# Weight codes of a decoder layer turned into weights on GpSimd instead of ScalarE

## The chip, the cores and the metric

One core of a Trainium2 chip runs the whole layer as one program. The metric is the device time of one execution in microseconds (us). TensorE (PE in the profile, PEld for its weight loads) multiplies, VectorE (DVE), ScalarE (ACT) and GpSimd (POOL) do the element-wise work, and SyncE (SP) issues DMAs. Each engine works off its own queue in order; an instruction waits for semaphores of others.

## The reference

A decoder layer on `x` of 2 x 512 x 1024 floats, in three parts, each with a residual:

```python
x = x + attn(layernorm(x))           # q, k, v, o weights from 4-bit codes
x = x + fq(layernorm(x)) @ fq(ctx)   # both sides rounded to 8-bit steps
x = x + layernorm(x) @ binarized(weight).T

# in attn: codes are int32 from 0 to 15, one scale per 128 rows and column
w = (codes.astype(float32) - 8.0) * repeat(scales, 128, axis=0)
q, k, v = x @ wq, x @ wk, x @ wv     # 32 query heads, 8 key/value heads of 128
# rotary embedding on even and odd elements of q and k, causal softmax, then
out = heads @ wo                     # 4096 x 1024 codes
```

## The kernel before

**Tiles.** The 1024 tokens lie along the free side, 512 for each batch. A column tile is one head's 128 columns of the query, key or value codes: 8 groups of 128 rows, brought as int32 by one DMA (`fetch_w`, L283, tile `st`) and turned into float32r weights `w` by subtracting 8 on ScalarE. There are 32 query, 8 key and 8 value tiles. Query and key tiles are turned in two halves (L294), the even and the odd columns, which puts the pairs of the rotary embedding in separate halves; a value tile takes one instruction (L291). A head's 128 rows of the output projection (`load_wo`, L304, tiles `sto` and `wo`) take one instruction too (L309).

**Scales.** They are not multiplied into the weights. A projection's sum `z` in PSUM is rescaled between two groups by the ratio of their scales (L368, on ScalarE, in place), and the last scale enters when the sum is read. So TensorE's group g+1 waits for ScalarE's L368 after group g. Each product is made of two passes, with the high and the low part of the input (`yH`, `yL`, L316).

**Around it.** Query and key sums are rotated by VectorE (L333 to L337). Attention of a head and batch: scores (L451), masked minimum on VectorE (L461), exponential on ScalarE (L466), division on VectorE (L470, L471), transposes (L493) copied by ScalarE (L498), values (L509), split into a high and a low part (L517, L519). The output projection (L316, `zo`, one PSUM buffer) is added into `accT` by VectorE (L432). Beside this the context is quantized and the last part's weight binarized on VectorE (L550 to L552, L579 to L587); their DMAs are issued by GpSimd (L564, L568, L577, L596) and wait for VectorE or ScalarE there. The later parts (from about 1000 us) read them back.

**Buffers and order.** `st` has 2 buffers, shared by column and output codes; `w` has 3, `wo` 2. The order of the steps is a written time line: `put(start, length, thunks)` places them at fractions of a unit (one head and batch), and a load stands LEAD = 0.7 units before its projection. From the sorted line a scheduler makes each engine's queue. The first three column tiles (`FIRST`: key 0, value 0, query 0) are loaded by hand at the start:

```python
sts = [fetch_w(*kc) for kc in FIRST[:2]]
...
ws[FIRST[0]] = load_w(*FIRST[0], sts[0])
...
ws[FIRST[1]] = load_w(*FIRST[1], sts[1])
projection(*FIRST[2])[0]()
```

Of the kernel before, what the change touches and what calls it, by code (L numbers as in the profile page):

```python
# [14 lines left out]
AF = mybir.ActivationFunctionType  # L15
ALU = mybir.AluOpType
# [7 lines left out]
HH = HD // 2  # L24
# [17 lines left out]
def decoder_layer(  # L42
# [20 lines left out]
    nc = tc.nc  # L63
# [217 lines left out]
    def fetch_w(kind, c):  # L281
        st = stp.tile([P, NK, HD], I32, tag="st", name="st")
        nc.sync.dma_start(st, codes[kind][:, :, c * HD : (c + 1) * HD])  # L283
        return st

    def load_w(kind, c, st=None):

        st = fetch_w(kind, c) if st is None else st
        w = wp.tile([P, NK, HD], F32R, tag="w", name="w")
        if kind == 2:  # L290
            nc.scalar.activation(w, st, AF.Copy, bias=-8.0)  # L291
        else:
            for e in range(2):
                nc.scalar.activation(  # L294
                    w[:, :, e * HH : (e + 1) * HH],
                    st.rearrange("p g (e two) -> p g two e", two=2)[:, :, e],
                    AF.Copy,
                    bias=-8.0,
                )
        return w  # L300

    def load_wo(h):
        st = stp.tile([P, D], I32, tag="st", name="sto")
        nc.sync.dma_start(st, o_codes[h * HD : (h + 1) * HD, :])  # L304
        if h == NH - 1:
            w = kvp.tile([P, D], F32R, tag="kT", name="wo")
        else:
            w = wop.tile([P, D], F32R, tag="wo", name="wo")
        nc.scalar.activation(w, st, AF.Copy, bias=-8.0)  # L309
        return w  # L310

    def product(z, lhsT, high, low, first=True, last=True):
# [30 lines left out]
    def projection(kind, c, bs=tuple(range(B))):  # L343
# [54 lines left out]
        def load():  # L398
            ws[kind, c] = load_w(kind, c)
# [20 lines left out]
    def out_projection(h):  # L420


        def tile_of(o):
            def run():
                hl = [[oHL[h, b][i] for b in range(B)] for i in range(2)]
                z = ps_z.tile([P, T], F32, tag="zo", name="zo", bufs=1)
                product(z, wo[h][:, o * P : (o + 1) * P], hl[0], hl[1])
                s = so[:, o, h : h + 1]
                if h == 0:
                    nc.scalar.activation(accT[o], z, AF.Copy, scale=s)  # L430
                else:
                    nc.vector.scalar_tensor_tensor(  # L432
                        accT[o], z, s, accT[o], ALU.mult, ALU.add
                    )

            return run

        def load():
            wo[h] = load_wo(h)

        return load, [tile_of(o) for o in range(NO)]
# [200 lines left out]
    ratios(sc1, ratio1, last1)  # L642
    turned[2][0]()
    ws[FIRST[0]] = load_w(*FIRST[0], sts[0])
    turned[2][1]()
    turned[3][0]()
    turned[3][1]()
    ws[FIRST[1]] = load_w(*FIRST[1], sts[1])
    projection(*FIRST[2])[0]()
    load_input(6)  # L650
# [305 lines left out]
```

## Time and profile before

| | before |
|---|---|
| median of three runs | 1229.86 us (1229.81 to 1230.28) |
| profiled execution, its span | 1229.79 us, 1228.0 us |
| granted TensorE clock | 0.994 |
| PE, DVE, ACT, POOL busy | 1189.5, 988.6, 856.5, 36.9 us |
| conversions of codes, on ACT | 88 of column tiles (60.2 us), 32 of the output projection (33.8 us) |

A row of the groups reads: line, engine, operation, what it writes and reads, shape and count, then busy time, mean duration of one in ns, the engine's idle time before it, and what ended that. TensorE's busy time is modelled and overlaps itself, so 97% does not mean that it never waits. A line of the waits reads: who waited for whom, microseconds in total, times, longest.

### The profile page before, as it was taken

Reading aid. Unit: us, or ns where it says so; the run is one execution under the profiler, and the core shown is the slowest. Engines: PE = TensorE matmul, PEld = TensorE weight load, DVE = VectorE, ACT = ScalarE, POOL = GpSimd, SP = SyncE. Lnnn points to the kernel's source line nnn. Section 1 sums busy time; section 2 is a strip of 40 time slices with the busy share of each in tenths; the row PEclk is TensorE's granted clock in tenths of the full one; section 3 lists DMA queues with packets and bytes.
Section 4 is the critical chain, followed back from the end, with each engine's and each line's share of the span. In section 5 each row is a group of like instructions: output and inputs, shape, how many; then the busy total and the mean of one; then the engine's idle time right before and its main releaser. Section 6 shows DMA issues by size and latency. Waiting matters only on the chain.

```text
span 1228.0 us, 14707 instructions
## 1 busy us (share of the span) xinstructions
PE 1189.5 (97%) x5022; PEld 801.2 (65%) x5030; DVE 988.6 (81%) x2035; ACT 856.5 (70%) x1767; POOL 36.9 (3%) x79
## 2 busy tenths in 40 slices
PE   5899999999999999999999999999999989899998
PEld 3557676667676777777767776777777666555443
DVE  6767889999999798979897889798979898955620
ACT  6899987877878777787778777877787744512310
POOL 1000000000000000000000000000000000000000
PEclk9999999999999999999999999999999989999999
DMA  7022222222122121212121212121212073110001
GB/s 246 1 92 85 69 69 86 69 69 65 56 71 85 61 78 44 69 61 77 61 77 44 69 61 78 61 76 45 69 61 73 25 239 102 42 36 35 18 24 45
DMA packets 75500, 85.69 MB, mean 70 GB/s; under 512 B 3073, under 2 KB 60801, under 8 KB 75425
## 3 DMA queue, kind: packets, MB, share of 16 engines
q1 hardware_dynamic: 69344, 63.64, 16.5%
q0 software_dynamic: 6080, 21.11, 4.7%
q8 instruction: 39, 0.64, 0.2%
q14 instruction: 37, 0.30, 0.1%
HBM read 72.16 MB, written 12.58 MB: 69 GB/s over the span
## 4 chain that ended last, share of the span: by engine, by line
PE 84%; DVE 8%; ACT 6%; issue 1%; DMA 1%; SPq 0%; POOL 0%; ACTq 0%
PE z L316 26%; PE zo L316 17%; PE o L509 11%; PE s L451 10%; PE m L875 9%; PE t L493 6%; ACT z L368 3%; PE m L843 2%; DVE accT L432 2%; DVE rot L333 1%; PE zb L316 1%; DVE accT L412 1%; DMA accT<-in_x 1%; PE vps L393 1%; DVE p L471 1%
## 5 line engine op out<-in xcount | busy, mean ns | idle before, releaser
L368 ACT ACTIVATE z<-z,ratio 128x512 f32<-128x512 f32 x672 | 423.7, 675 | 75.2 <-PE z L316 74.0
L316 PE MATMUL z<-yH,w 128*128 128x512 f32 x768 | 348.9, 460 | 7.8 <-ACT z L368 5.1
L432 DVE SCALAR_TENSOR_TENSOR accT<-zo,so,accT 128x1024 f32<-128x1024 f32 x224 | 286.5, 1279 | 55.7 <-PE zo L316 54.0
L316 PE MATMUL z<-yL,w 128*128 128x512 f32 x768 | 313.5, 416 | 0.0
L316 PEld LDWEIGHTS z<-yH,w 128*128 128x128 f32 x768 | 144.5, 189 | 92.0 <-ACT z L368 60.1
L316 PE MATMUL zo<-oH,wo 128*128 128x512 f32 x464 | 200.5, 432 | 1.4 <-DVE accT L432 0.8
L316 PE MATMUL zo<-oL,wo 128*128 128x512 f32 x464 | 184.7, 398 | 0.0
L466 ACT ACTIVATE p<-p,low 128x128 f32<-128x128 f32 (+3 forms) x256 | 143.9, 565 | 54.7 <-DVE low L461 51.8
L451 PE MATMUL s<-kT,q 128*128 128x128 f32 (+3 forms) x512 | 173.6, 439 | 0.0
L316 PEld LDWEIGHTS z<-yL,w 128*128 128x128 f32 x768 | 145.3, 189 | 25.7 <-issue 7.2
L509 PE MATMUL o<-pt,v 128*128 128x512 f32 (+3 forms) x512 | 149.9, 434 | 0.1
L333 DVE SCALAR_TENSOR_TENSOR rot<-z,last,sin 64x512 f32<-64x512 f32 x160 | 120.0, 750 | 23.3 <-PE z L316 19.8
L509 PEld LDWEIGHTS o<-pt,v 128*128 128x128 f32 x512 | 96.3, 189 | 60.3 <-issue 30.7
L461 DVE CUSTOM_DVE_ANT_0 p<-s,mask 128x128 f32<-128x128 f32 (+3 forms) x256 | 121.2, 482 | 14.8 <-PE s L451 13.4
L498 ACT COPY pt<-t 128x512 f32<-128x512 f32 (+3 forms) x256 | 105.4, 442 | 21.6 <-PE t L493 20.5
L493 PE MATMUL t<-ident,p 128*128 128x128 f32 x640 | 117.3, 278 | 2.7 <-DVE oL L519 2.0
L316 PEld LDWEIGHTS zo<-oH,wo 128*128 128x128 f32 x464 | 87.3, 188 | 42.9 <-DVE accT L432 22.7
L875 PE MATMUL m<-bwT,y2T 128*128 128x512 f32 x256 | 111.3, 592 | 0.0
L451 PEld LDWEIGHTS s<-kT,q 128*128 128x128 f32 x512 | 89.5, 190 | 28.7 <-ACT pt L498 2.3
L493 PEld LDWEIGHTS t<-ident,p 128*128 128x128 f32 x640 | 79.3, 141 | 36.4 <-ACT pt L498 8.1
L316 PEld LDWEIGHTS zo<-oL,wo 128*128 128x128 f32 x464 | 87.6, 189 | 17.1 <-issue 2.6
L471 DVE TENSOR_SCALAR p<-p,inv 128x128 f32<-128x128 f32 (+3 forms) x256 | 95.3, 382 | 2.3
(129 smaller groups left out, 1050.8 us busy)
## 6 DMA issues: line engine op xcount, KB each, us to landing
st<-in_L_attn_q_codes SPq DMA_DIRECT2D x32, 512.0 KB, 4.0
sto<-in_L_attn_o_codes SPq DMA_DIRECT2D x32, 512.0 KB, 3.3
ctx<-in_ctx POOLq DMA_DIRECT2D x16, 512.0 KB, 3.6
accT<-in_x SPq DMA_DIRECT2D x8, 512.0 KB, 6.3
st<-in_L_attn_k_codes SPq DMA_DIRECT2D x8, 512.0 KB, 3.7
st<-in_L_attn_v_codes SPq DMA_DIRECT2D x8, 512.0 KB, 3.8
wt<-in_L_ffn_weight POOLq DMA_DIRECT2D x8, 512.0 KB, 3.8
bwd<-wT POOLq DMA_DIRECT2D x8, 512.0 KB, 2.9
```

Of the source, the lines that this page charges most:

```text
L316: nc.tensor.matmul(z[:, b * S : (b + 1) * S], lhsT, rhs[b], start=first and part == 0, stop=last and part == 1, skip_group_check=True,)
L333: nc.vector.scalar_tensor_tensor(t[to], z[of_], s[of_], sin[of_], ALU.mult, ALU.mult)
L368: nc.scalar.activation(z, z, AF.Copy, scale=ratio_[:, g + 1 : g + 2])
L432: nc.vector.scalar_tensor_tensor(accT[o], z, s, accT[o], ALU.mult, ALU.add)
L451: nc.tensor.matmul(ps[:, :n], q[:, b * S + i * P : b * S + n], k[:, b * S : b * S + n], start=True, stop=True,)
L461: nc.vector.tensor_tensor_reduce(p[:, :n], ps[:, :n], mask[:, S - n :], -1.0, -MASKED, ALU.add, ALU.min, accum_out=low,)
L466: nc.scalar.activation(p[:, :n], p[:, :n], AF.Exp, bias=low, scale=-1.0, accum_out=total)
L471: nc.vector.tensor_scalar(p[:, :n], p[:, :n], inv, None, ALU.mult)
L493: nc.tensor.transpose(ps[:, (i - j) * P : (i - j + 1) * P], probs[h, b][i][:, j * P : (j + 1) * P], ident,)
L498: nc.scalar.copy(ptq[h, b][j], ps[:, :n])
L509: nc.tensor.matmul(ps[:, j * P :], v[:, b * TB + j, :], pt[j], start=(j == 0), stop=(j == TB - 1),)
L875: nc.tensor.matmul(ps, yTs[m][:, k, :], late["bwT"][:, k, c], start=(k == 0), stop=(k == NK - 1))
```

## The change

The conversions are issued to GpSimd, as an addition of -8 and a multiplication by 1, where the tile was not fetched beforehand; all of the output projection's are. The split in halves stays. Behind `load_w` every line stands one lower in the changed kernel (L316 is L317 there, L368 is L369); the conversions are its L298, L300 and L310.

```diff
     def load_w(kind, c, st=None):
 
+        early = st is not None
         st = fetch_w(kind, c) if st is None else st
         w = wp.tile([P, NK, HD], F32R, tag="w", name="w")
         if kind == 2:
-            nc.scalar.activation(w, st, AF.Copy, bias=-8.0)
+            parts = [(w, st)]
         else:
-            for e in range(2):
-                nc.scalar.activation(
-                    w[:, :, e * HH : (e + 1) * HH],
-                    st.rearrange("p g (e two) -> p g two e", two=2)[:, :, e],
-                    AF.Copy,
-                    bias=-8.0,
-                )
+            both = st.rearrange("p g (e two) -> p g two e", two=2)
+            parts = [(w[:, :, e * HH : (e + 1) * HH], both[:, :, e]) for e in range(2)]
+        for to, codes_ in parts:
+            if early:
+                nc.scalar.activation(to, codes_, AF.Copy, bias=-8.0)
+            else:
+                nc.gpsimd.tensor_scalar(to, codes_, -8.0, 1.0, ALU.add, ALU.mult)
         return w
 
     def load_wo(h):
...
-        nc.scalar.activation(w, st, AF.Copy, bias=-8.0)
+        nc.gpsimd.tensor_scalar(w, st, -8.0, 1.0, ALU.add, ALU.mult)
         return w
```

## The prediction

> **What bounds the kernel now.** I read the page first: busy time and the chain that ended last.
>
> ```profile
> PE 1189.5 (97%) x5022; PEld 801.2 (65%) x5030; DVE 988.6 (81%) x2035; ACT 856.5 (70%) x1767; POOL 36.9 (3%) x79
> PE 84%; DVE 8%; ACT 6%; issue 1%; DMA 1%; SPq 0%; POOL 0%; ACTq 0%
> ```
>
> TensorE (PE) carries 84% of the path, and no edit here touches it. What an engine swap can win or lose lies in the 6% on ScalarE (ACT, 74 us) and the 8% on VectorE (DVE, 98 us). Then the busy time by stretch (columns: PE, PEld, DVE, ACT, POOL, each with its count, then clock and DMA):
>
> ```profile
> 60.00:100.00 40.00, 37.84 (x153) 23.79 (x152) 29.89 (x75) 39.72 (x83) 1.60 (x3) 1.00 0.28 85
> 100.00:140.00 40.00, 39.97 (x184) 28.75 (x182) 29.71 (x64) 39.45 (x77) 1.08 (x2) 1.00 0.24 78
> 400.00:700.00 300.00, 299.38 (x1307) 214.73 (x1305) 258.04 (x532) 236.76 (x504) 8.62 (x16) 1.00 0.20 64
> ```
>
> ScalarE is full from 60 to 140 us (79.2 of 80). In the long middle it is 79% busy (237 of 300), VectorE 86%, and GpSimd (POOL) idle. Next the groups by shape: what moves, the rows nearest to its new price, and VectorE's largest group that works from SBUF to SBUF.
>
> ```profile
> L294 ACT ACTIVATE w<-st 128x512 fp32r<-128x512 int32 x80 | 51.6, 678 | 7.4 <-PE z L316 5.7 <-DMA st<-in_L_attn_k_codes 1.3
> L309 ACT ACTIVATE wo<-sto 128x1024 fp32r<-128x1024 int32 x32 | 33.8, 1056 | 4.0 <-PE zo L316 4.0
> L291 ACT ACTIVATE w<-st 128x1024 fp32r<-128x1024 int32 x8 | 8.6, 1069 | 2.3 <-PE z L316 2.3
> L805 POOL TENSOR_SCALAR v<-mv 128x1 f32<-128x1 f32 x8 | 1.8, 221 | 196.0 <-DVE mv L92 196.0
> L77 POOL MEMSET mask<- 128x384 f32 x1 | 0.4, 422 | 0.0
> masks.py:30 POOL TENSOR_SCALAR_AFFINE_SELECT mask<-mask 128x128 f32<-128x128 f32 x1 | 0.3, 312 | 0.0
> L471 DVE TENSOR_SCALAR p<-p,inv 128x512 f32<-128x512 f32 x64 | 30.9, 482 | 1.0
> ```
>
> Last, who waits: TensorE's weight loader for ScalarE's rescaling in 60 to 140 us, the same in 140 to 990 us (total, times, longest), and then all that TensorE waited for the paired conversions of L294 in the whole run.
>
> ```profile
> PEld z L316 <- ACT z L368: 6.8, 20, 0.9
> ...
> PEld z L316 <- ACT z L368: 40.2, 138, 0.7
> ...
>   PEld z L316: 1.9, 3
>   PE z L316: 0.6, 1
> ```
>
> The weights themselves are hardly ever late. What is late is the rescaling L368, which shares ScalarE with the conversions.
>
> **What moves.** Only tiles handed in with their codes stay on ScalarE. That is two tiles, the first key and value tile: the third of FIRST is loaded by its projection without codes, so it goes to GpSimd although the change is said to spare three. Moved are 32 query and 7 key tiles in two halves each (78 instructions), 7 value tiles and 32 output tiles (39 of 128x1024). ScalarE loses 78 x 0.678 + 7 x 1.069 + 32 x 1.056 = 94 us by the mean durations.
>
> **What ScalarE's relief is worth.** On the chain, window by window, the moved conversions make eleven pieces, 8.1 us in all (59.28, 80.74, 191.9, 242.26, 340.35, 378.7 and 979.1 us among their starts). By stage:
> - 20 to 60 us: the third tile's conversion ends on ScalarE at 24.52 and TensorE uses it at 24.57. Its codes are requested at 16.60 and such a transfer takes 4.0 us, so GpSimd can finish near 22.5. Behind it ScalarE's rescalings are next late: 0.5 us won, at most 1.1.
> - 60 to 140 us: 10.35 us of conversions leave a full ScalarE (5.92 + 3.30 + 1.13). TensorE's waits on ScalarE there come to about 11 us, but it is itself close to full after 100 us. I take half, 5 us; bounds 0 and 10. Here weights have little lead (the tile at 80.62 is used at 81.91), so a slower conversion shows: 1 us back.
> - 140 to 990 us: 78.2 us leave (42.41 + 29.44 + 6.36), 12% of ScalarE's work. TensorE waits for ScalarE here for some 55 us (40.2 for L368, the rest for copies). In proportion 12% of it, 6.5 us, is won. Bounds: 4, what the chain itself holds here, and 15, if queueing falls faster than load.
> - The last three output tiles: the piece at 979.1 is 1.06 us; its slack is 13 us on GpSimd. 1 us.
> Gain 0.5 + 5 - 1 + 6.5 + 1 = 12 us; bounds 4 and 26.
>
> **What GpSimd takes.** The trace has no large GpSimd arithmetic. Lower bound, the two memsets: (422 - 205) / 256 = 0.85 ns an element, so 0.53 us for 512 and 0.96 for 1024. Upper, the select in full proportion, 300 ns for 128 elements: 1.2 and 2.4 us. I take 221 ns fixed (L805) and 1.0 ns an element, 0.75 and 1.25 us, as most of the select's 300 looks fixed. In all 78 x 0.75 + 39 x 1.25 = 107 us (79 to 187), 12% of the 890 us from 100 to 990.
>
> The Trainium skill, page "GPSIMD Engine Reference", section "3.1 Elementwise — side-by-side cycle accounting", gives simple one-input bodies 1.03 cycles an element and a good loop 1.8 at 1.2 GHz: by it, an estimate, 1024 elements take 0.9 to 1.5 us, inside my bounds, and its advice is still to keep elementwise work off GpSimd.
>
> **Where slower conversions are covered.** From 140 us on, almost every tile is converted 19 to 43 us before TensorE's first use (one at 402.41 to 403.69 is used at 430.56), because its slot and not its need starts it. A conversion half a microsecond longer costs nothing there. If that cover were gone, 1 us for each of these 60-odd tiles would be some 60 us.
>
> **The queues.** GpSimd issues 54 DMAs, and conversions now stand behind those that wait: its stores wait up to 31.8 us for VectorE's L552. In the built program the conversion next behind such a store has its first use 25 us or more after the store's time in this trace, so nothing is late; 0 us, at most 12 for one store that comes 12 us beyond the cover. Its own DMAs wait for a conversion, 1.25 us at most, with their readers far off: 0 to 2 us. SyncE's next code transfers wait for GpSimd instead of ScalarE (L283, L304): same slots, same cover, 0. TensorE's order hardly changes after 140 us; a reshuffle is 2 us either way.
>
> **What VectorE pays.** GpSimd and VectorE now work on SBUF together, which this trace shows only for GpSimd's DMA issues: there, L471 at 128x512 took 483 ns against 482 without. Lower bound 0. Upper: each of the 1577 VectorE instructions from 100 to 990 us waits out a conversion that it meets: 1577 x 12% x 0.49 us (mean rest: the squared durations summed, over twice their sum) = 93 us. I take it for those with all large operands in SBUF, 256 L471, 80 L337 and some 88 of the weight and context preparation, 424 in all: 424 x 0.12 x 0.49 = 25 us. VectorE carries 98 of its 989 busy us on the path, 10%; for added time on an engine already 88% busy I double it: 20%, 5 us. Bounds 0 and 25, or more with slower conversions.
>
> The Trainium skill, page "SBUF — State Buffer", section "Who interferes with whom", speaks against this change: GpSimd shares a port pair with VectorE's two-port and two-input instructions, and the later one blocks fully. No row here shows it; by that rule the 25 us stand, and by the unchanged 483 ns of L471 alone they would be 0 and the time 1217.5.
>
> **Sum.** The profiled execution took 1229.8 us (span 1228.0 and 1.8 around it), as the median 1229.86. 1229.8 - 12 + 5 = 1222.8; of the 12 I hold back 3, since waits that one engine frees are partly met again by the next (VectorE's accumulation at L432 holds TensorE's loader for 22 us already). Forecast 1225.5.
>
> **Rivals.**
> 1. VectorE becomes the late engine: slower. Mechanism: it stands still while a conversion runs, in the softmax's L471 and the rotation's L337. At the upper durations (1.2 and 2.4 us) GpSimd works 187 us, 21%, and the mean rest is 0.90 us: 424 x 0.21 x 0.90 = 80 us on an engine that has 12% of 850 idle, so it is full. At 30% on the path that is 24, less 9 to 12 gained: 1242 to 1245; at 45%, 1255. At my 20% it decides once the delay passes 60 us, which is a 128x1024 conversion of about 1.9 us. For it: VectorE's 86 to 88%, and TensorE's single zo buffer behind it. Against: softmax has a unit of lead.
> 2. Relief and blocking cancel: 1227.5 to 1232. For: conversions stand mostly in ScalarE's idle places after 140 us, so removing them frees little.
> 3. No blocking: 12 us gained in full and nothing paid, 1217.5 (bounds 1214 to 1221).
> 4. GpSimd's queue holds weights back: 12 us for each late store. Against: the 25 us of margin.
>
> **How the numbers follow.** Forecast case 0.37 (own range 1220 to 1227.3), rival 3 0.09, so faster 0.46. Rival 2 0.15, same. Rival 1 0.36 and rival 4 0.03, slower 0.39. 0.2%, 2.5 us, is about what a measurement of this kernel can tell from no change. The range leaves out the tail above 1248 (0.13) and below 1215 (0.06).
>
> **What would show it.** Right: ScalarE near 763 us busy, 60 to 140 us shorter, TensorE's wait for L368 in the middle under 36 us, GpSimd some 107 us in 117 conversions of 0.75 and 1.25 us, L471 longer on average by under 0.1 us. Wrong: a 128x1024 conversion over 1.9 us, VectorE over 92% in the middle, more TensorE waits on L432 or L471 than ScalarE's gave back, or TensorE waiting for w or wo after 140 us.

## The result, and the profile after

The changed kernel takes 1235.94 us (median of 4, 1234.76 to 1237.28); the kernel before, on the same chip, 1230.07 us. The ratio is 1.0047, 95% interval 1.0031 to 1.0063: slower by 5.9 us, where 4.3 us of gain were forecast. The profiled execution took 1237.28 us, its span 1235.2 us.

Busy time and the chain of the page after. The shares of this chain add up to 77% only, so nothing is read from it but that GpSimd's arithmetic is not on it.

```profile
PE 1190.5 (96%) x5030; PEld 800.8 (65%) x5030; DVE 995.2 (81%) x2035; ACT 780.4 (63%) x1650; POOL 133.4 (11%) x196
PE 65%; DVE 9%; ACT 1%; issue 1%; DMA 1%; POOL 0%; ACTq 0%; POOLq 0%
```

ScalarE (ACT) lost 76 us, as meant, and TensorE works as long as before. The stretches after (PE, PEld, DVE, ACT, POOL, clock and DMA):

```profile
60.00:100.00 40.00, 38.13 (x155) 24.05 (x154) 29.80 (x70) 35.86 (x74) 10.62 (x14) 1.00 0.36 109
100.00:140.00 40.00, 38.01 (x170) 27.02 (x169) 28.27 (x65) 35.33 (x69) 4.87 (x7) 1.00 0.21 67
400.00:700.00 300.00, 297.83 (x1302) 212.06 (x1301) 258.09 (x533) 211.30 (x467) 36.84 (x52) 1.00 0.20 64
```

ScalarE is no longer full from 60 to 140 us (71.2 of 80), and in the middle VectorE is no busier (258.09 against 258.04). But TensorE does 38.0 us of work from 100 to 140 us where it did 40.0. The groups by shape: the conversions in their new place, and the two VectorE groups that were to suffer.

```profile
L300 POOL TENSOR_SCALAR w<-st 128x512 fp32r<-128x512 int32 x78 | 53.1, 681 | 386.0 <-PE z L317 254.1 <-issue 109.8 <-DMA st<-in_L_attn_q_codes 19.6
L338 DVE TENSOR_TENSOR q<-q,rot 128x512 f32<-128x512 f32 x64 | 46.9, 734 | 0.1
L310 POOL TENSOR_SCALAR wo<-sto 128x1024 fp32r<-128x1024 int32 x32 | 34.9, 1090 | 228.5 <-issue 149.7 <-PE zo L317 72.5 <-DMA sto<-in_L_attn_o_codes 6.2
L472 DVE TENSOR_SCALAR p<-p,inv 128x128 f32<-128x128 f32 x64 | 19.0, 296 | 0.7
L300 POOL TENSOR_SCALAR w<-st 128x1024 fp32r<-128x1024 int32 x7 | 7.3, 1041 | 76.2 <-PE z L317 64.1 <-DVE rot L334 6.2 <-issue 5.9
```

A conversion is as quick on GpSimd as it was on ScalarE. What is new stands behind the second bar: GpSimd stands idle in front of its conversions for 386, 228 and 76 us, of which 254, 72 and 64 until TensorE (`z`, `zo`) has done with a weight buffer, and everything behind them in its queue waits too. Now the waits: TensorE's loader for ScalarE in 60 to 140 us and in 140 to 990 us; TensorE's for the softmax division L472 in 140 to 990 us; then two lines that the profile before does not have, VectorE's waits for loads (the last one of the whole run).

```profile
PEld z L317 <- ACT z L369: 8.2, 26, 0.9
...
PEld z L317 <- ACT z L369: 38.2, 133, 0.7
...
PEld t L494 <- DVE p L472: 5.6, 10, 2.4
...
PE t L494 <- DVE p L472: 2.6, 3, 2.0
...
DVE ctx L551 <- DMA ctx<-in_ctx: 2.3, 2, 1.8
...
DVE wsum L580 <- DMA wt<-in_L_ffn_weight: 3.4, 2, 2.2
```

Before, the division was L471, and TensorE's wait for it in 140 to 990 us stood in one line:

```profile
PEld t L493 <- DVE p L471: 1.4, 5, 0.4
```

The relief of ScalarE hardly shows (6.8 and 40.2 us before). VectorE now stands still for loads of context and weight, which GpSimd issues: 5.7 us in four pauses. And TensorE waits 8.2 us for the division where it waited 1.4, which the prediction had named as a sign of its being wrong. One of the pauses in the timeline (start, duration, engine, line, operation, idle before). Before, on GpSimd:

```profile
108.30 0.54 POOL L596 DMA_DIRECT2D bwd<-wT  x1 [25.59 <-ACT pt L498]
112.14 0.54 POOL L577 DMA_DIRECT2D wt<-in_L_ffn_weight  x1 [3.29 <-PE z L316]
```

After, on GpSimd, then on VectorE and on TensorE:

```profile
109.98 0.57 POOL L597 DMA_DIRECT2D bwd<-wT  x1 [0.25 <-ACT wT L595]
128.08 1.40 POOL L300 TENSOR_SCALAR w<-st 128x512 fp32r<-128x512 int32 x2 [17.53 <-PE z L317]
130.43 1.04 POOL L310 TENSOR_SCALAR wo<-sto 128x1024 fp32r<-128x1024 int32 x1 [0.96 <-PE zo L317]
131.53 0.56 POOL L578 DMA_DIRECT2D wt<-in_L_ffn_weight  x1
...
138.47 1.22 DVE L580 TENSOR_REDUCE wsum<-wt 128x1 f32<-128x1024 f32 x1 [2.18 <-DMA wt<-in_L_ffn_weight]
...
140.14 0.44 PE L494 MATMUL t<-ident,p 128*128 128x128 f32 x2 [1.97 <-DVE p L472]
```

The load stands behind a conversion that waits 17.5 us for its buffer, so it goes out at 131.5 instead of 112.1 us. VectorE, in order, pauses 2.2 us for it; the softmax division behind the pause is late, and TensorE waits 2.0 us for that. Over all 24 loads the median time from issue to VectorE's first read fell from 22.0 to 6.4 us, and a transfer takes about 5.

**Lags.** To place the loss I compare profiles at equal work: the time by which TensorE has done a given amount of matmul work (each matmul counted with one fixed time for its shape), less that time in the profile before. The columns e5 to e18 are experiments of the next section. The first 10 us, where the kernels are alike, already differ by 0 to 3 us between executions, so only steps after 100 us are read.

| us | after | e17 | e13 | e18 | e5 | e7 |
|---|---|---|---|---|---|---|
| 100 | 2.1 | 2.2 | 7.1 | 6.6 | 1.1 | 6.4 |
| 156 | 5.9 | 2.4 | 8.6 | 6.3 | 3.3 | 9.3 |
| 275 | 4.1 | 0.4 | 8.8 | 6.8 | 1.2 | 8.9 |
| 430 | 8.7 | 2.9 | 10.6 | 6.8 | 1.9 | 8.9 |
| 965 | 8.8 | 2.1 | 11.5 | 6.6 | 1.0 | 12.2 |

The changed kernel loses 6.7 us between 100 and 430 us (8.8 - 2.1), in jumps at its pauses, and nothing after.

### The profile page after: what moved, and what is told of

The parts are those of the page before. It is cut to its first block, busy times and chain, and to the rows that moved or that the text cites. A ratio compares the mean times of both kernels' runs of the same rounds, so it can differ in the third digit from the quotient of the medians.

```text
span 1235.2 us, 14775 instructions
## 1 busy us (share of the span) xinstructions
PE 1190.5 (96%) x5030; PEld 800.8 (65%) x5030; DVE 995.2 (81%) x2035; ACT 780.4 (63%) x1650; POOL 133.4 (11%) x196
## 4 chain that ended last, share of the span: by engine, by line
PE 65%; DVE 9%; ACT 1%; issue 1%; DMA 1%; POOL 0%; ACTq 0%; POOLq 0%
PE z L317 19%; PE zo L317 14%; PE m L876 9%; PE o L510 8%; PE s L452 7%; PE t L494 4%; DVE rot L334 2%; PE m L844 2%; DVE accT L433 2%; PE zb L317 1%; DVE accT L413 1%; DVE p L472 1%; DVE p L462 1%; ACT z L369 1%; DVE stats L90 0%
## 5 line engine op out<-in xcount | busy, mean ns | idle before, releaser
L369 ACT ACTIVATE z<-z,ratio 128x512 f32<-128x512 f32 x672 | 423.0, 672 | 109.7 <-PE z L317 108.8
L317 PE MATMUL z<-yH,w 128*128 128x512 f32 x768 | 350.7, 463 | 8.0 <-ACT z L369 5.1
L433 DVE SCALAR_TENSOR_TENSOR accT<-zo,so,accT 128x1024 f32<-128x1024 f32 x224 | 286.5, 1279 | 54.8 <-PE zo L317 52.3
L317 PE MATMUL z<-yL,w 128*128 128x512 f32 x768 | 312.7, 417 | 0.0
L317 PEld LDWEIGHTS z<-yH,w 128*128 128x128 f32 x768 | 145.0, 190 | 92.4 <-ACT z L369 58.2
L317 PE MATMUL zo<-oH,wo 128*128 128x512 f32 x464 | 200.3, 432 | 1.6 <-DVE accT L433 1.0
L317 PE MATMUL zo<-oL,wo 128*128 128x512 f32 x464 | 185.7, 400 | 1.3 <-DVE oL L520 1.3
L317 PEld LDWEIGHTS z<-yL,w 128*128 128x128 f32 x768 | 146.0, 190 | 25.7 <-issue 6.7
L334 DVE SCALAR_TENSOR_TENSOR rot<-z,last,sin 64x512 f32<-64x512 f32 x160 | 120.0, 750 | 19.7 <-PE z L317 16.0
L317 PEld LDWEIGHTS zo<-oH,wo 128*128 128x128 f32 x464 | 87.7, 189 | 41.2 <-DVE accT L433 21.7
L300 POOL TENSOR_SCALAR w<-st 128x512 fp32r<-128x512 int32 (+1 forms) x85 | 60.4, 710 | 462.2 <-PE z L317 318.2
L317 PEld LDWEIGHTS zo<-oL,wo 128*128 128x128 f32 x464 | 87.8, 189 | 19.1 <-issue 2.8
```

What stands on the lines that cost most here:

```text
L300: nc.gpsimd.tensor_scalar(to, codes_, -8.0, 1.0, ALU.add, ALU.mult)
L317: nc.tensor.matmul(z[:, b * S : (b + 1) * S], lhsT, rhs[b], start=first and part == 0, stop=last and part == 1, skip_group_check=True,)
L334: nc.vector.scalar_tensor_tensor(t[to], z[of_], s[of_], sin[of_], ALU.mult, ALU.mult)
L369: nc.scalar.activation(z, z, AF.Copy, scale=ratio_[:, g + 1 : g + 2])
L433: nc.vector.scalar_tensor_tensor(accT[o], z, s, accT[o], ALU.mult, ALU.add)
```

## The experiments

### The change again, and parts of it

**e1**, the changed kernel without an edit.

> The changed kernel once more, unchanged, for a second profile of it. In the first one 2.5 us of the loss stand in the first 10 us, where a load of scales landed at 10.34 instead of 7.53 us with nothing changed ahead of it. If that is chance of the transfer, this profile shows the landing near 7.5 again and a time of 1233 to 1235; if it belongs to the change, the landing stays near 10.3 and the time at 1236 to 1237. The stretched VectorE instructions (18, 6.2 us) and the VectorE pauses for GpSimd's loads (5.7 us at 138, 282, 407 and 753 us) should come back in both cases.

1236.74 us, ratio 1.0053 (1.004 to 1.0066), in the upper of the two ranges expected. The scales landed at 9.37 us, between the two cases; without any conversion on GpSimd they landed at 8.83 (e9) and 10.16 us (e12), so that difference is chance. The pauses stand at the same loads (2.27 us at 137, 1.07 at 279, 2.58 at 405), so they are no accident of one execution.

**e4**, only the last three output tiles on GpSimd.

```diff
-        nc.gpsimd.tensor_scalar(w, st, -8.0, 1.0, ALU.add, ALU.mult)
+        if h >= NH - 3:
+            nc.gpsimd.tensor_scalar(w, st, -8.0, 1.0, ALU.add, ALU.mult)
+        else:
+            nc.scalar.activation(w, st, AF.Copy, bias=-8.0)
```

> The kernel before with only the last three output tiles (heads 29 to 31) converted on GpSimd. Beyond 985 us the profile of the changed kernel caught up 3.3 us on the one before. If that gain comes from these three conversions leaving ScalarE's and TensorE's path there, this kernel takes 1226.5 to 1228.5 and pays nothing, since nothing is queued behind them earlier. If the gain was only the lag being taken up by idle time at the end, 1229.5 to 1230.5.

1229.96 us, ratio 0.9997 (0.9988 to 1.0006): the 1 us promised for the tail does not show.

**e8**, only the 32 output tiles on GpSimd (L300 back on ScalarE).

> The change for the 32 output tiles alone; all column tiles stay on ScalarE. GpSimd then works 35 us instead of 95. In the changed kernel eight of the stretched VectorE instructions (L338, 0.25 us each) meet an output tile's conversion and ten meet a column tile's. Theory C: a third to a half of the loss, 1232 to 1233.5. Theory Q: an output tile's conversion waits for its buffer as long as a column tile's, and the loads behind it come late: VectorE's pauses stay at 3 us or more, 1232 to 1234. Of the two, the profile tells by stretch and pauses.

1231.72 us, ratio 1.0012 (1.0004 to 1.0021), with one pause (1.24 us at 137) and a median lead of the loads of 9.0 us. With fewer conversions in front of the loads the loss is smaller.

### What ScalarE's conversions are worth

**e7**, the kernel before, with each conversion done twice on ScalarE (the value tiles' too).

```diff
...
-        nc.scalar.activation(w, st, AF.Copy, bias=-8.0)
+        for _ in range(2):
+            nc.scalar.activation(w, st, AF.Copy, bias=-8.0)
```

> The kernel before with every conversion but for the value tiles' done twice on ScalarE, some 85 us more there, to see what ScalarE's load is worth at all. Theory R, the prediction's (waits on the rescaling go with ScalarE's load): 6 us more from 140 to 990 us and 5 to 8 us more from 60 to 140, 1241 to 1245. Theory N (the rescaling's waits are the length of the way from TensorE through ScalarE and back, ScalarE has room): nothing from 140 to 990 us, and only the stage from 60 to 140 us, where ScalarE is full, grows, 1232 to 1237.

1241.69 us, ratio 1.0097 (1.0084 to 1.011). The total lies where the prediction's own theory put it (1241 to 1245), but the split by stages does not fit that theory. By the lags 7.6 us were lost by 156 us (9.3, against 1.7 at 10 us), mostly where ScalarE is full, and 2.9 from there to 965. In 140 to 990 us ScalarE's busy time rose from 668 to 735 us, by 67, for these 3 us; the proportion that I had used makes such a step worth some 6. e7 bounds the relief from one side; the relief alone, without conversions elsewhere, was not tried.

### What GpSimd's conversions cost by themselves

**e3**, each conversion twice on GpSimd; **e6**, each in pieces of 256 elements.

```diff
                 nc.gpsimd.tensor_scalar(to, codes_, -8.0, 1.0, ALU.add, ALU.mult)
+                nc.gpsimd.tensor_scalar(to, codes_, -8.0, 1.0, ALU.add, ALU.mult)
...
```

```diff
...
-        nc.gpsimd.tensor_scalar(w, st, -8.0, 1.0, ALU.add, ALU.mult)
+        for j in range(0, D, 256):
+            nc.gpsimd.tensor_scalar(
+                w[:, j : j + 256], st[:, j : j + 256], -8.0, 1.0, ALU.add, ALU.mult
+            )
```

> The changed kernel with every conversion on GpSimd done twice in a row, 97 us more of GpSimd arithmetic. Theory C: VectorE's stretch doubles from 6 to 12 us or more, and the time rises by another 4 to 7 us, to 1240 to 1243. Theory Q: what holds the loads back is the wait of a conversion for its buffer and not its length, so at most 1 us more for each late load, 1236 to 1239.

> The changed kernel with every conversion on GpSimd cut into pieces of 256 elements, so that a VectorE instruction that meets one waits for 0.3 us at most and not for the rest of 0.65 to 1.1 us. Theory C: VectorE's stretch falls from 6 to 2 or 3 us and 2 us of the time come back, 1234 to 1235, the pauses for loads staying. If a VectorE instruction has to wait for the whole run of pieces, or more pieces mean more meetings, the stretch stays at 6 us or rises and so does the time, 1236 to 1240. Theory Q: 1236 to 1237, as the queue is as long as before.

e3: 1250.66 us, ratio 1.017 (1.0156 to 1.0184), above what either theory allowed. Both suspects grew: VectorE's pauses for loads to 7.45 us, and its instructions stretched by a conversion from 18 (6.2 us in all) to 48 (20.6 us). So it does not tell them apart, and the part of its loss that goes to each was not traced. e6: 1236.33 us, ratio 1.0055 (1.0043 to 1.0067): 33 stretched instructions, 5.4 us in all; shorter pieces hold VectorE up less each time but meet it more often.

### Moving the loads

**e2**, all 24 loads issued by ScalarE; **e5**, by GpSimd but 0.6 units earlier in the time line; **e9**, these early loads in the kernel before; **e10**, as e5 with the weight loads on ScalarE; **e11**, as e5 with all loads there.

```diff
-            nc.gpsimd.dma_start(c, context[b, t * P : (t + 1) * P, :])
+            nc.scalar.dma_start(c, context[b, t * P : (t + 1) * P, :])
...
-            nc.gpsimd.dma_start(w, weight[t * P : (t + 1) * P, :])
+            nc.scalar.dma_start(w, weight[t * P : (t + 1) * P, :])
```

```diff
     def weight_ahead(t):
...
-            w = row_tile("wt")
-            nc.gpsimd.dma_start(w, weight[t * P : (t + 1) * P, :])
+            w = held.pop(t)
...
+    loads = [weight_load(t) for t in range(NK)]
+    loads += [context_load(b, t) for b in range(B) for t in range(NK)]
+    put(2 - 0.6, 57, loads)
```

> The changed kernel with the 24 loads of the context and of the last part's weight issued by ScalarE instead of GpSimd, so that they no longer stand behind conversions that wait for a buffer or for codes. Theory Q (these loads come late and VectorE's queue stops on them): the pauses before L551 and L580 go, 3 to 5 us come back, 1231 to 1233. Theory C (the shared port: VectorE waits out conversions): no change against the changed kernel, 1235 to 1237, since conversions and VectorE's work are as before. ScalarE's queue has some 24 x 0.4 us more to issue, which no theory charges.

> The changed kernel with the 24 loads of the context and of the last part's weight placed 0.6 units (some 9 us) earlier in the time line than the work on them, still issued by GpSimd. In the changed kernel the median load is issued 6.4 us before VectorE reads it, before the change 22 us. Theory Q (late loads stop VectorE): the lead is back above 10 us, the pauses of 4 to 6 us go, the time falls by about half of them, to 1233 to 1234.5. Theory C (shared port alone): VectorE's stretch of 6 us stays and the time too, 1235.5 to 1237. A third buffer of the common pool is held longer, which could cost the rotation a wait of up to 2 us.

> The kernel before, with only the 24 loads of context and weight 0.6 units earlier in the time line; no conversion on GpSimd. Tells whether the early loads brought e5 back because they undo the loss of the GpSimd change, or because they speed any kernel. Theory (loss by late loads): in the kernel before no load was late (no pause of VectorE behind one after 13 us), so 1228.5 to 1231.5, within 0.2% of before. Rival A (the early placement is a gain by itself, worth some 6 us, and it only covers a loss of another kind): 1222 to 1226. Rival B (it costs something, by the time that row tiles are held): 1232 to 1236.

> The changed kernel with the early loads of e5, and the eight weight loads issued by ScalarE instead of GpSimd; this is meant to take away the pause of 2.16 us at 137 us that e5 kept, where a weight load stood behind a conversion until 130.5. Theory (pauses behind late loads are what is left): 1227.5 to 1229.5, with no pause of VectorE at 137 us. Rival (that pause is taken up by other slack of the early stage, or ScalarE's queue makes the load late as well): 1229.5 to 1231.5.

> As e10, and the sixteen context loads issued by ScalarE too, so that GpSimd's queue holds no load that VectorE reads. Theory: no pause of VectorE behind a load over 0.5 us is left, and the time is that of e10 or up to 1 us less: 1227 to 1229.5. Rival (ScalarE's queue makes some loads late where GpSimd's did not, as with the plain loads on ScalarE): 1230 to 1234.

e2: 1235.20 us, ratio 1.0042 (1.003 to 1.0055), where I had expected 1231 to 1233 if late loads were the loss. ScalarE's queue is in order as well: the lead is 7.2 us, the pause at 138 is gone, three of 1.0 to 1.6 us are there at 277, 403 and 749. e5: 1230.29 us, ratio 1.000 (0.9991 to 1.0008): the whole loss is back, with 13 instructions of VectorE still stretched by 4.1 us. But that does not show what I meant it to show: the median lead is 6.8 us, where I had expected over 10, and three pauses for loads are left (2.16 us at 138, 0.91 at 159, 0.82 at 908). What brought e5 back is not settled; its order is another one, as the next part says. e9: 1231.60 us, ratio 1.0006 (0.9997 to 1.0015), so early loads are no gain by themselves. e10: 1231.13 us, ratio 1.0003 (0.9995 to 1.0012), with pauses of 0.9, 2.0 and 1.0 us left, and e11: 1234.58 us, ratio 1.003 (1.0017 to 1.0042): the gains I expected of them did not come. In e11 TensorE falls back by some 3 us in small steps from 468 to 946 us with no pause for a load over 0.5 us there. So it does in e2, and not in e10 (3.4 to 3.0 us of lag): it goes with the context loads on ScalarE; by what way stays open.

**e12**, the kernel before, where GpSimd reads one column of each converted tile.

```diff
...
+        nc.gpsimd.tensor_scalar(seen_, w[:, 0:1].bitcast(F32), -8.0, 1.0, ALU.add, ALU.mult)
```

> The kernel before, where GpSimd reads one column of each tile that ScalarE has converted (all but the first two; 80 small instructions of some 0.2 us, whose results nobody uses). GpSimd's queue then waits for each conversion as in the changed kernel, and so do the loads behind it, but it takes nothing from ScalarE and holds VectorE up for almost no time. Theory (the loss is the queue's wait): the loads' lead falls from 22 us to under 12, VectorE pauses for loads come back, and the time is 1233 to 1237. Rival (the loss is VectorE's stretched instructions): lead as short, and 1230 to 1231.5. If the lead stays near 22 us the run tells nothing on either.

1231.38 us, ratio 1.0006 (0.9997 to 1.0015), where I had expected 1233 to 1237. The lead fell to 10.5 us, but only one pause over 0.4 us came of it: 1.08 us at 98 us, where the lag steps up by 0.94. A shorter lead cost nothing there as long as the load still landed in time, and this pause was paid nearly in full. Not every pause is: e9 has two, 1.34 us at 157 and 1.12 at 277, and its lag is 1.0 us ahead of both and behind both. So e12 does not show the whole loss, and the sum of the pauses is not the loss.

### Holding the order

The scheduler gives the changed kernel another order: with the two sequences aligned, 384 of TensorE's 5022 matmuls stand elsewhere than before, and 847 in e5. e5 could owe its gain to that. So the next runs force an order, by edges between neighbours that wait for nothing:

```diff
+        for a, b in zip(order[:-1], order[1:]):
+            tc.add_manual_dep(
+                ours[b], ours[a].name,
+                mybir.DependencyInfo(mybir.DependencyClass.NoSync, mybir.DependencyReason.DATA),
+                reason="held_order",
+            )
```

**e13**: the changed kernel in the old order. **e14**: the kernel before in the new order. **e15** and **e16**: early loads and conversions on GpSimd, in the new and in the old order.

> The changed kernel, its conversions on GpSimd, with the instructions of TensorE, VectorE and ScalarE held in the order that they have in the kernel before (edges between neighbours, no waits). Tells the loss by late loads from a loss by the new order that the scheduler chose (about 9% of TensorE's rows stand elsewhere). Theory (late loads behind GpSimd's conversions): the loss stays, 1233 to 1238, with VectorE pausing for context or weight. Rival (order): 1229 to 1231.5.

> The kernel before, conversions on ScalarE, with TensorE, VectorE and ScalarE held in the order of the changed kernel. Theory (late loads): 1229 to 1231.5, no pause of VectorE. Rival (order): 1234 to 1237.

> The changed kernel with the early loads of e5, but TensorE, VectorE and ScalarE held in the order of the changed kernel, so that only the place of the loads in GpSimd's queue differs from it. Theory (late loads): the gain of e5 stays, 1229 to 1232. Rival (e5 won by its own order of the other engines): 1234 to 1237.

> Conversions on GpSimd, the early loads of e5, and TensorE, VectorE and ScalarE held in the order of the kernel before. Theory (late loads) and rival (order) both say 1229 to 1231.5; under 1228 would be a gain by ScalarE's relief that no run so far has shown, over 1233 a cost of the conversions that is neither order nor load.

| | us | ratio (interval) | pauses of VectorE for loads, over 0.5 us |
|---|---|---|---|
| e13 | 1240.53 | 1.0084 (1.0071 to 1.0096) | 1.73 at 144, 1.78 at 287, 0.67 at 756 |
| e14 | 1242.65 | 1.0098 (1.0084 to 1.0112) | none |
| e15 | 1235.95 | 1.0043 (1.003 to 1.0056) | 2.82 at 139, 0.76 at 283 |
| e16 | 1241.78 | 1.0091 (1.0077 to 1.0105) | 2.26 at 144, 1.63 at 288 |

None of the four settles it; e13, e14 and e16 lie above the ranges of both theories, and e15 lies in the rival's. An order is made around one kernel's own costs, and a foreign one is dear: e14 loses 12 us without a load being late, for reasons not followed further. e15 loses as the changed kernel does, which speaks for the order, except that in the held order the pauses are there as well and the early loads had not become early where it counts: the one of 131 us was still issued at 131.68, behind the same conversion. e13 explains its first 5.3 us itself. TensorE and GpSimd there (lines stand some 90 further down in this kernel; L400 is the conversion L310):

```profile
88.69 0.30 PE L318 MATMUL sps<-ident,sraw 128*128 128x128 f32 x1 [4.42 <-DMA sraw<-in_L_attn_o_scales]
...
82.74 1.58 POOL L400 TENSOR_SCALAR wo<-sto 128x1024 fp32r<-128x1024 int32 x1 [3.40 <-DMA sto<-in_L_attn_o_codes]
84.38 1.09 POOL L294 DMA_DIRECT2D sraw<-in_L_attn_o_scales  x2
```

The scales of the output projection are GpSimd's load too. Before they went out at 69 and 70 us; here they stand behind a conversion until 84.4, and TensorE waits 4.4 us for them: the same mechanism with another victim.

### Only the loads' place in GpSimd's queue

**e17** is the changed kernel with every engine's order held as it is there, SyncE's too; only each of the 24 loads stands ahead of the conversions directly before it in GpSimd's queue. **e18** does the same to e13. Of GpSimd's held order, where the second weight load stands:

```diff
 L597 bwd<-wT
+L578 wt<-in_L_ffn_weight
 L300 w<-st x2
 L310 wo<-sto
-L578 wt<-in_L_ffn_weight
```

> The changed kernel with the order of every engine held as it is there (SyncE's too), except that in GpSimd's queue each of the 24 loads of context and weight stands ahead of the conversions directly before it (1 to 6 of them, for 23 loads). e15 had left the loads at 131 and 278 us behind conversions, so that its pauses of 2.8 and 0.8 us stayed. Theory (late loads): the pauses at 138, 282 and 407 us go, which took some 4 to 5 us from TensorE: 1230.5 to 1233; what is then left above the kernel before is the new order's. Rival (the new order and the stretched instructions cost it all): 1234.5 to 1237.5.

> e13 (conversions on GpSimd, the order of the kernel before on TensorE, VectorE and ScalarE) with the 24 loads moved ahead in GpSimd's queue as in e17. Theory (late loads): its pauses of 1.7, 1.8 and 0.7 us go and 3 to 4.5 us come back, 1236 to 1238; the 5.3 us that e13 lost between 78 and 100 us, where no load is late, stay. Rival (loads do not matter): 1239.5 to 1241.5.

e17: **1230.50 us**, ratio 0.9996 (0.9987 to 1.0005). e18: 1235.48 us, ratio 1.0042 (1.0029 to 1.0054), 5.1 us less than e13. GpSimd in e17, and VectorE's read of the same load (lines stand 99 further down in this kernel; L677 is the load L578, L679 its first read L580):

```profile
110.05 0.57 POOL L696 DMA_DIRECT2D bwd<-wT  x1 [0.29 <-DVE kT L436]
114.31 0.54 POOL L677 DMA_DIRECT2D wt<-in_L_ffn_weight  x1 [3.69 <-PE z L416]
128.14 1.38 POOL L399 TENSOR_SCALAR w<-st 128x512 fp32r<-128x512 int32 x2 [13.30 <-PE z L416]
...
136.28 1.20 DVE L679 TENSOR_REDUCE wsum<-wt 128x1 f32<-128x1024 f32 x1
```

The load goes out at 114.3, lands long before it is read, and the read has no idle time before it. The median lead is 21.8 us again (22.0 before), and one pause of 0.3 us is left. The conversions are all still on GpSimd, ScalarE is as light as in the changed kernel (780.5 us busy), 18 VectorE instructions are stretched by 5.4 us, TensorE's wait for the division from 140 to 990 us is 3.0 us instead of 8.2, and the new order is unchanged. Its lag is 2.2 us at 100 and 2.1 at 965, where the changed kernel's goes from 2.1 to 8.8. The jumps that are missing are 3.6 us at 118 to 156, 0.8 at 275 to 296, 1.3 at 389 to 410 and 0.7 at 585 to 601 us. So the loss is that of loads standing behind conversions, but for the last piece, where a stretched instruction lay (below). That the order is held is no gain by itself: e15 holds TensorE, VectorE and ScalarE to the same order, but leaves the load of 131 us behind its conversion, and takes 1235.95.

No run beats the kernel before; e4, e5, e9, e10, e12 and e17 equal it within their intervals.

## Why the prediction was wrong

**The step that failed** is the sentence on GpSimd's queue: "Its own DMAs wait for a conversion, 1.25 us at most, with their readers far off: 0 to 2 us." I priced the wait by a conversion's duration. A load behind it waits for what the conversion itself waits for, a weight buffer, for up to 25 us; I had counted that same early start as the cover of the conversions. And the readers were far off only because loads had gone out early: a lead of 22 us before, 6.4 after. That term is 5.4 us (1235.9 less e17's 1230.5; 6.3 by the ratios to the kernel before on the same chip, 1.0047 less 0.9996), 0.7 of it a stretched instruction's; in the old order it is 5.1 (e13 less e18), and the scales' 5.3 on top. I had looked at that queue for weights held back (rival 4), not for what the weights hold back.

**The relief of ScalarE was mis-sized**: 12 us forecast, 9 after what was held back, and no gain measured. In e17 relief, stretched instructions and new order together are worth nothing (ratio 0.9996).
- 60 to 140 us: 5 us forecast. The lag moves from 2.4 to 2.2 us between 55 and 118 us although ScalarE has room now, and TensorE's wait for L369 is 8.2 us where it was 6.8.
- 140 to 990 us: 6.5 us forecast, in proportion to ScalarE's load. The wait for the rescaling went from 40.2 to 38.2 us, not under 36, and in 430 to 990 us from 24.4 to 23.9. I read most of such a wait as the rescaling's own 0.67 us between two groups, which a lighter ScalarE does not shorten; that was not tried apart. In e18, in the old order, the lag is 6.5 us at 137 and 6.5 at 987: there ScalarE has 605 us of work for 668, VectorE 5.4 us of stretching, and together they are worth nothing. So the relief there is at most what the stretching cost, and that is 5.4 us if all of it was paid.
- The tail's 1 us is not seen in e4.

**ScalarE's busy time** fell by 76 us, not 94: its instructions overlap, so the sum of durations overstates what leaves (e7 added 93 us by durations and 79.5 of busy time; before, the durations of all ScalarE instructions add up to 1000 us and the busy time to 856.5).

**GpSimd's conversions** were about right: 95.3 us (53.1 + 7.3 + 34.9) for 107 forecast, 0.68 and 1.04 to 1.09 us for 0.75 and 1.25. The estimate worked out from the Trainium skill, page "GPSIMD Engine Reference", section "3.1 Elementwise — side-by-side cycle accounting", was 0.9 to 1.5 us for the larger, which agrees. Right were also the third tile, which went to GpSimd against the words of the change, and the cover of the weights: after 140 us TensorE waits for no tile.

**VectorE's payment** was right in kind and too high: 18 stretched instructions and 6.2 us, for 25 forecast. Of the 5 us that I put on the path, 0.7 is seen. The case that I gave most of the slower side, rival 1, is not what happened: VectorE was no busier in the middle (258.1 us of 300). One of its signs did come, TensorE's longer wait for the softmax division (8.2 us for 1.4), but with the loads ahead of the conversions (e17) it is 3.0, with as many stretched instructions.

**The order** changed more than "hardly changes after 140 us" says: 261 of the 384 matmuls that moved stand between 140 and 990 us. As a sum it did no harm: e17, in the new order, ends where the kernel before does. That single orders can be worth 12 us I had not seen.

**The sum** has a slip: 1222.8 and 3 make 1225.8, not 1225.5, and 1229.8 less 12 is 1217.8, not 1217.5. It changes nothing in the outcome.

## What to carry to other kernels

Work moved to an engine that issues DMAs goes into their queue: price a load behind it by the longest wait in front of it, the buffer that the moved instruction waits for included, and compare with the lead that the load has now. If work must go there, put the loads ahead of it in that queue; here that alone was worth 5.4 us. And take a wait for a busy engine as a gain only if the wait gets shorter with the engine's load: half of one stage's waits and a proportional part of another's were guesses here, and no gain came of either.

## What the hardware showed beside that

**A conversion takes about as long on GpSimd as on ScalarE**: 681 and 1090 ns at 512 and 1024 elements, against 678 and 1056. From e6's 448 ns at 256 elements (every second one read) the step to 512 is 0.91 ns an element; the pieces read in a row took 444.

**Who begins first decides.** The rotation L338 takes 685 ns alone, 970 on average where a conversion was already running (11 of them), and 685 where it began before the conversion (3). One such meeting, on VectorE and on GpSimd:

```profile
206.03 1.32 DVE L338 TENSOR_TENSOR q<-q,rot 128x512 f32<-128x512 f32 x1
...
205.77 1.03 POOL L300 TENSOR_SCALAR w<-st 128x1024 fp32r<-128x1024 int32 x1 [5.89 <-issue]
```

Its 1.32 us are the conversion's rest (205.77 + 1.03 - 206.03 = 0.77) and most of its own 0.69. The instructions looked at that read one operand from PSUM did not pay: L433 1277 ns in 14 meetings against 1279, L334 747 in 31 against 749. This is what the Trainium skill states, page "SBUF — State Buffer", section "Who interferes with whom": only two-input and two-port instructions of VectorE meet GpSimd, and the one that comes later waits. One stretched division at 601 us (1106 ns for 414) came out on TensorE as a lag of 0.7 us, in e1, with 1106 ns at the same place, as well; the eight meetings of L338, 0.25 us each, from 460 us on did not.

**A load that goes out together with another travels more slowly.** GpSimd's context loads, in the changed kernel and in e17 (KB each, median us to landing):

```profile
ctx<-in_ctx POOLq DMA_DIRECT2D x16, 512.0 KB, 5.0
...
ctx<-in_ctx POOLq DMA_DIRECT2D x16, 512.0 KB, 3.7
```

The conversion that lets the load go also frees a code buffer, and SyncE sends the next 512 KB of codes at the same moment (402.59 and 402.62 us in one case). Of the 24 loads of the changed kernel 20 go out within 0.5 us of such a transfer, and take 5.1 us in the median; before it was 3. In e17 none goes out within 1.6 us of one; 15 still overlap with one for over 1 us, and the median is 3.7. This is a part of the loss that the late issue alone does not explain. The load issued at 131.53 us took 6.9 us; VectorE stood ready for it at 136.3, and with 3.7 us it would have landed at 135.2. By the same estimate two more of the four pauses would be gone, and the one of 1.8 us at 407 would be 0.7. No run tested the two apart.
